# New costs, latencies and conflict units in the list scheduler of a four-layer kernel

## The chip, the cores and the metric

The kernel runs on one core of a Trainium2 chip. The metric is the device time of one execution in microseconds. A NeuronCore has a matrix engine (TensorE, PE in the profile), VectorE (DVE), ScalarE (ACT), GpSimd (POOL) and a queue that issues transfers (SyncE, SP). Each engine works through its own queue in the order in which the program was written, and semaphores make one engine wait for another. The order of each queue is therefore fixed when the program is built.

## The reference, cut to what matters

The input is x, 8 samples of 256 channels by 32 x 32 positions. Four layers follow one another:

```
layer 0: x += gamma1 * attention(rmsnorm(x))        4 heads, keys of 32, values of 64, 1024 positions,
                                                    softmax, a 3x3 depthwise convolution of v added
         x += gamma2 * ffn(rmsnorm(x))              1x1 to 1024, depthwise 3x3, gelu(x1)*x2, 1x1 to 256,
                                                    an 8x8 FFT filter
layer 1: x += attention(groupnorm(x))               8 heads of 32, softmax; then a small gelu MLP
layer 2: quantised 1x1 -> 3x3 -> 1x1 convolutions with a residual
layer 3: a selective scan in four directions (rows, columns, each forward and backward):
         xc, z = split(u W_in);  xc = silu(conv4(xc));  dt, B, C = projections of xc
         h[t] = h[t-1] * exp(dt[t] A) + dt[t] B[t] xc[t]    512 channels x 16 states
         y[t] = sum_s h[t,s] C[t,s];  out = (y + D xc) silu(z) W_out;  the four outputs are added
```

## The kernel before, in words

The kernel has two phases. `phase_a` computes layers 0 to 2, `phase_b` layer 3. Within a phase nothing is a plain loop: the work is written as Python generators ("strands"), and a list scheduler, the class `_Order`, decides in which order their instructions are emitted.

**The list.** A strand yields an `_Op` (one instruction) or a list of them (a group that stays together). `run()` computes for every ready strand when its next group could start (`start()`): when the engine is free, when each operand was last written, and, for what is written, last read. Data from another engine count as usable `LATENCY` after they are finished. The strand with the earliest start is emitted, ties going to the smaller rank, and the engine's free time advances by the group's cost. So the prices in `_Op.__init__` and the latencies shape a simulated timeline at build time, and the order of every queue comes out of it. The chip itself is not told of these times.

**Conflict units.** `_Op.blocks` says which part of a tile an operand touches, in units of 64 elements of a partition for tiles of up to 512 elements, and of 512 for larger ones. Two operands of one tile that share a unit are treated as conflicting in the list.

**Rooms.** Buffers come from rooms (`_Room`). A strand waits until a room has a free buffer; the buffer's earliest use is when its last reader ended, plus a latency (`put`). The PSUM room of `phase_a` is `bank`, with 8 banks; while an attention is running, everything else together may hold three of them (`OTHERS`).

**Fillers.** `keep_dense` runs ahead of every group for PE. It adds up the rows that PE has worked in the last 3.4 us of simulated time. If that is under half of full, it emits filler matmuls (a constant `minus` tile, 128 x 512, priced at 0.22 us, line 277 in the profile) into a free bank. Their purpose is to keep PE's activity up, since the granted clock depends on it. Before the change it may emit as many as fit between the time at which PE is free and the later of two times: the group's expected start, and 0.66 us after PE is free.

**phase_a.** The eight samples run as strands; a sample begins when the one three before it has finished `layer0`. `layer0`, `feed_forward`, `layer1` and `layer2` are the linear parts. `maxima` makes scores in one direction to get each query's maximum and sum: pairs or quads of matmuls into banks (tile names `bank<-big,big`), then for each bank a TENSOR_REDUCE on DVE into one column of `stats` (`least`), then an exponential on ACT with that column as bias, summed into another column of `stats` (`sums`). A `stats` tile has 128 elements to a partition. `exponentials` makes the scores again in the other direction, subtracts maximum and log-sum with a small matmul, takes the exponentials (`exps`), and `values` multiplies them with v.

**phase_b.** The sequence work is cut into 64 blocks (8 samples, 4 directions, 2 halves) with 16 states each: 1024 groups. For each group ACT makes four `dbu` (dt B x, scaled) and four `da` (exp of dt A), PE transposes the `dbu` into `db`, DVE runs four scans into `h` (two to a tile), ACT copies the last column to `st` in the first half of a direction, POOL multiplies `h` by C (`cb`), and PE transposes and sums the products into `py`. The strands `decays`, `scales`, `turns`, `scans`, `ends`, `products` and `sums` do this; `ahead` brings in the projections, convolutions and activations of the blocks to come. `da` has 5 buffers, `dbu` 12, `h` 6 pairs, `db` 3 banks.

Of the kernel before, what the change touches and what calls it, by code (L numbers as in the profile page):

```python
# [20 lines left out]
F32 = mybir.dt.float32  # L21
# [78 lines left out]
class _Op:  # L100


    def __init__(self, engine, method, args, kw):
        self.engine, self.method, self.args, self.kw = engine, method, args, kw
        out, ins = args[0], [a for a in (*args[1:], *kw.values()) if isinstance(a, bass.AP)]
        self.reads = {k for a in ins for k in self.blocks(a)}
        self.writes = {k for a in (out, kw.get("accum_out")) if a is not None for k in self.blocks(a)}
        self.landing = 0.0
        n = max(math.prod(a.shape[1:]) for a in (out, *ins)) / 1024
        near = all(a.space == out.space and out.space != PSUM for a in ins)  # L110
        points = sum(math.prod(a.shape[1:]) == 1 for a in ins)
        if engine == "tensor":
            x = kw.get("rhs", ins[0])
            n = math.prod(x.shape[1:]) / 1024
            self.rows = x.shape[0] / P * n * (0.44 if x.dtype != F32 else 1.72)
            move = method == "transpose" or kw.get("is_transpose", False)
            self.cost = max(0.06, (0.22 if x.shape[0] < 20 else 0) + n * (0.96 if move else 0.44 if x.dtype != F32 else 1.76 if n > 0.2 else 2.0))
            self.rows *= 0.5 if move else 1
        elif engine == "vector":
            fast = near and method in ("tensor_scalar", "tensor_copy")  # L120
            both = near and method == "tensor_tensor"
            three = near and method == "scalar_tensor_tensor"
            if method == "tensor_tensor_scan":
                self.cost = 0.03 + 2.15 * n + 0.05 * points
            elif both or three:
                self.cost = 0.04 + 1.5 * n
            elif fast:
                self.cost = 0.04 + 0.9 * n
            else:
                self.cost = 0.05 + 1.09 * n + 0.05 * points  # L130
        elif engine == "scalar":
            self.cost = 0.05 + 0.06 * near + 0.85 * n + 0.093 * points + 0.17 * ("accum_out" in kw)
        elif engine == "gpsimd":
            self.cost = 0.12 + 2.2 * n if method == "tensor_tensor" else 0.07 + (2.0 if out.dtype == BF16 else 1.5) * n
        else:
            self.cost, self.landing = 0.1, 3.0

    @staticmethod
    def blocks(a):
        step = max(1, a.ap[0][0])  # L140
        lo = a.offset % step
        hi = lo + sum((n - 1) * abs(s) for s, n in list(a.ap)[1:])
        unit = 64 if step <= HALF else HALF
        return [(a.name, k) for k in range(lo // unit, hi // unit + 1)]

    def emit(self, nc):
# [37 lines left out]
class _Order:  # L184
# [2 lines left out]

    LATENCY = 0.35  # L190

    def __init__(self, nc):
        self.nc, self.strands, self.n = nc, [], 0
        self.free, self.written, self.read, self.base, self.last = {}, {}, {}, {}, {}
        self.rooms, self.minus, self.way, self.rows, self.fresh = [], None, 0.0, [], {}

    def add(self, rank, strand):
        self.n += 1
# [30 lines left out]

    def put(self, room, t):  # L230
        k = room.of[t.name]
        end = [v[0] for d in (self.written, self.read) for v in d.pop(t.name, {}).values()]
        self.last[room.tag, k] = max(end + [0.0]) + self.LATENCY
        room.put(t)

    def start(self, ops):
        e = ops[0].engine
        t = self.free.get(e, 0.0)
        for o in ops:
            for k in o.reads | o.writes:  # L240
                t = max(t, self.base.get(k[0], 0.0))
                w, by = self.written.get(k[0], {}).get(k, (0.0, e))
                t = max(t, w + (self.LATENCY if by != e else 0.0))
            for k in o.writes:
                w, by = self.read.get(k[0], {}).get(k, (0.0, e))
                t = max(t, w + (self.LATENCY if by != e else 0.0))
        return t

    WINDOW, DENSE, DUMMY = 3.4, 0.5, 0.22

    def keep_dense(self, t, cost, ops):

        work = sum(o.rows for o in ops)
        free, end = self.free.get("tensor", 0.0), t + cost
        self.rows = [r for r in self.rows if r[1] > end - self.WINDOW]
        seen = sum(w * (b - max(a, end - self.WINDOW)) / (b - a) for a, b, w in self.rows)
        n = math.ceil((self.DENSE * self.WINDOW - seen - work * min(1.0, self.WINDOW / cost)) / self.DUMMY)
        n = max(n, math.ceil((t - free - self.DENSE * self.WINDOW) / self.DUMMY))
        if n > 0:
            since, room, k = min(  # L260
                ((self.last.get((r.tag, k), 0.0), j, k) for j, r in enumerate(self.rooms) for k in r.left),
                default=(1e9, 0, 0),
            )
            x = self.fresh.get(ops[0].args[0].name)
            if x is not None and self.base[x.name] < since:
                since, room = self.base[x.name], None
            begin = max(free, since)
            n = min(n, int((max(t, free + 0.66) - begin) / self.DUMMY))
            if since < 1e9 and n > 0:
                if room is not None:  # L270
                    room = self.rooms[room]
                    room.left.remove(k)
                    room.left.insert(0, k)
                    x = room.take()
                rhs = self.minus.unsqueeze(1).to_broadcast([P, 4, P])
                for _ in range(n):
                    self.nc.tensor.matmul(x, lhsT=self.minus, rhs=rhs, start=True, stop=True)  # L277
                if room is not None:
                    room.put(x)
                    self.last[room.tag, k] = begin + n * self.DUMMY + self.LATENCY  # L280
                self.rows.append((begin, begin + n * self.DUMMY, n * self.DUMMY))
                t = max(t, begin + n * self.DUMMY)
        self.rows.append((t, t + cost, work))
        return t

    def run(self):
        while self.strands:
# [12 lines left out]
            cost, ops = s[2]  # L300
            e = ops[0].engine
            if self.rooms and e == "tensor":
                t = self.keep_dense(t, cost, ops)
            for o in ops:
                o.emit(self.nc)
                for k in o.reads:
# [9 lines left out]
def phase_a(ctx, tc, i, col, ident, codes, w_parts):  # L316
# [18 lines left out]
    order = _Order(nc)  # L335
    NBIG, NMID, NLOW = 12, 9, 7
    OTHERS = 3
    MAXIMA, SCORES = 2, 1.12
    GATE = 1
    big = _Room(rooms, "big", NBIG, [P, CC, N])  # L340
    mid = _Room(rooms, "mid", NMID, [P, N])
# [241 lines left out]
    def maxima(rank, q, k, rows, done):  # L583
# [6 lines left out]
        def some():  # L590
            while todo:
# [9 lines left out]
                for e in range(n):  # L601
# [1 line left out]
                    ops.append(  # L603
                        T.matmul(bb[e], lhsT=q[r, t * P : (t + 1) * P], rhs=k[r, hs(j)], start=True, stop=True)
                    )
                yield (0.9, ops)
                for e in range(n):
                    m, s = (x[:, j, t, h + e : h + e + 1] for x in (least, sums))
                    yield V.tensor_reduce(m, bb[e], AX.X, ALU.max, negate=True)
# [496 lines left out]
        def emit(self, nc):  # L1106
            nc.scalar.preload_act_table_set("natural_log_exp_and_others")

    order.rooms, order.minus, order.way = [bank], minus, 0.05
    stage = [0] * B  # L1110

    def sample(b):
# [670 lines left out]
```

## Time and profile before

| | |
|---|---|
| median of 3 runs | 10249.33 us (10241.9 to 10274.5) |
| profiled execution | 10256.65 us, span 10254.8 us |
| mean granted PE clock | 0.977 |
| busy share of the span | PE 93%, ACT 83%, DVE 75%, POOL 60% |
| filler matmuls (line 277) | 2805, of these 1749 into `bank`, in `phase_a` |

Almost every instruction is emitted by one helper, `_Op.emit`, on line 147, so groups are told apart by engine, operation and tile names. In a group's line come the count, the busy time and the mean of one in ns, then the idle time of the engine just before them and what ended it. Ends of matmuls are modelled, so a busy PE can still be a PE that waits a little; the distance from one start to the next says more. A float32 matmul is recorded as two.

### The profile page before, as it was taken

The page shows a single profiled execution, that of the slowest core. Times are in us where ns is not written, and L with a number is a line of the kernel's source. Part 1 is how long each engine was busy: PE and PEld are TensorE (multiplying, and loading weights), DVE is VectorE, ACT ScalarE, POOL GpSimd, SP SyncE. Part 2 cuts the span into 40 slices and gives each one's busy share as a digit, 9 for nine tenths or more (in the row PEclk, how much of TensorE's full clock was granted, in tenths as well). Part 3 has the DMA queues.
Part 4 walks back from the last instruction along what each step waited for, and adds up shares of the span by engine and source line. Part 5 has one row for each costly group of instructions (what it writes and reads, how often), then busy time and mean ns, then how long its engine had stood idle before and what let it go on. Part 6 is the DMA issues. An engine that isn't in the chain of part 4 may idle for free.

```text
span 10254.8 us, 153646 instructions
## 1 busy us (share of the span) xinstructions
PE 9573.8 (93%) x57349; PEld 5920.9 (58%) x57349; DVE 7741.9 (75%) x8671; ACT 8521.2 (83%) x15873; POOL 6150.3 (60%) x2993
## 2 busy tenths in 40 slices
PE   9999999999999989999999999999999999999998
PEld 3333333333333347777777777777777776777776
DVE  6366557585666448887888888888888888888788
ACT  7867676767666759988998999898999899898898
POOL 1433132242121038877887878787878787787788
PEclk9998999999999999999999999999999999999999
DMA  2100000000000002112111112111111211111111
GB/s 59 30 19 17 21 22 18 17 22 17 17 17 9 17 29 54 52 47 57 44 55 55 47 51 59 44 55 50 54 51 49 55 54 45 59 50 49 55 46 54
DMA packets 219630, 416.06 MB, mean 41 GB/s; under 512 B 25137, under 2 KB 67505, under 8 KB 213762
## 3 DMA queue, kind: packets, MB, share of 16 engines
q1 hardware_dynamic: 218882, 406.24, 13.7%
q8 instruction: 451, 7.39, 0.3%
q14 instruction: 297, 2.43, 0.1%
HBM read 358.43 MB, written 37.22 MB: 39 GB/s over the span
## 4 chain that ended last, share of the span: by engine, by line
ACT 28%; PE 22%; DVE 10%; issue 2%; POOL 1%; DMA 1%; DVEq 0%; SPq 0%; POOLq 0%; ACTq 0%
ACT da L147 11%; ACT dbu L147 10%; PE pp L147 9%; DVE h L147 8%; PE py L147 7%; PE db L147 6%; ACT L147 2%; ACT xs L147 1%; ACT dt L147 1%; DMA wi<-w_in 1%; POOL h L147 1%; ACT L156 1%; DVE ys L147 1%; ACT st L147 1%; ACT z L147 0%
## 5 line engine op out<-in xcount | busy, mean ns | idle before, releaser
L147 POOL TENSOR_TENSOR h<-h,cb 128x1024 f32<-128x1024 f32 x2048 | 4814.7, 2375 | 1013.8 <-DVE h L147 422.9
L147 ACT ACTIVATE da<-dt,am 128x512 f32<-128x512 f32 x4096 | 2863.9, 714 | 506.0 <-DVE h L147 502.0
L147 ACT ACTIVATE dbu<-du,bT 128x512 f32<-128x512 f32 x4096 | 2783.4, 709 | 17.1 <-PE db L147 10.4
L147 DVE TENSOR_TENSOR_SCAN h<-da,db 128x512 f32<-128x512 f32 x2048 | 2342.4, 1202 | 467.1 <-ACT da L147 201.5
L147 DVE TENSOR_TENSOR_SCAN h<-da,st,db 128x512 f32<-128x512 f32 x2048 | 2466.0, 1262 | 224.8 <-ACT da L147 131.3
L147 PE MATMUL db<-ident,dbu 128*128 128x128 f32 x16384 | 2329.7, 276 | 194.7 <-DVE h L147 157.7
L147 PEld LDWEIGHTS db<-ident,dbu 128*128 128x128 f32 x16384 | 1855.6, 141 | 798.8 <-DVE h L147 350.4
L147 PE MATMUL py<-ident,h 128*128 128x128 f32 x16384 | 2099.2, 274 | 95.4 <-POOL h L147 90.0
L147 PEld LDWEIGHTS py<-ident,h 128*128 128x128 f32 x16384 | 1837.4, 141 | 236.4 <-POOL h L147 179.2
L147 DVE TENSOR_REDUCE stats<-bank 128x1 f32<-128x512 f32 x1536 | 987.9, 684 | 655.0 <-PE bank L147 652.2
L147 ACT ACTIVATE bank<-bank,stats 128x512 f32<-128x512 f32 x1536 | 1024.7, 672 | 409.2 <-DVE stats L147 395.3
L147 POOL TENSOR_TENSOR mid<-mid,mid 128x961 f32<-128x961 f32 (+2 forms) x192 | 394.6, 2062 | 1115.5 <-ACT mid L147 591.9
L147 PE MATMUL bank<-big,big 32*128 32x512 f32 x4096 | 928.3, 667 | 15.7 <-ACT bank L147 9.0
L147 ACT ACTIVATE exps<-bank 128x512 f32<-128x512 f32 x1536 | 796.9, 620 | 166.4 <-PE bank L147 158.9
L147 PE MATMUL pp<-xi,cvd 128*128 128x512 f32 x1488 | 692.6, 601 | 1.6 <-DVE ys L147 1.6
L277 PEld LDWEIGHTS <-minus 128*128 128x128 bf16 x2805 | 260.6, 101 | 663.4 <-issue 463.8
L147 DVE SCALAR_TENSOR_TENSOR mid<-mid,cols,mid 128x961 f32<-128x961 f32 (+1 forms) x384 | 595.6, 1551 | 6.1
L277 PE MATMUL bank<-minus 128*128 128x512 bf16 x1749 | 508.5, 414 | 52.5 <-ACT bank L147 41.1
L147 PEld LDWEIGHTS bank<-big,big 32*128 32x128 f32 x4096 | 283.2, 191 | 463.0 <-issue 267.4
L147 PE MATMUL bank<-exps,big 128*32 128x512 f32 (+1 forms) x3072 | 543.8, 613 | 0.3 <-ACT exps L147 0.3
L147 POOL TENSOR_TENSOR tmp<-dt,xs 128x512 f32<-128x512 f32 x256 | 322.6, 1274 | 298.2 <-ACT dt L147 227.0
L147 POOL TENSOR_TENSOR big<-big,mid 128x992 f32<-128x992 f32 (+1 forms) x128 | 324.4, 2542 | 290.1 <-ACT mid L147 287.4
(207 smaller groups left out, 9389.5 us busy)
## 6 DMA issues: line engine op xcount, KB each, us to landing
cb<-c_d SPq DMA_DIRECT2D x1024, 256.0 KB, 3.3
wi<-w_in SPq DMA_DIRECT2D x192, 192.0 KB, 3.6
big<-in_x_dram SPq DMA_DIRECT2D x16, 1024.0 KB, 5.2
kept<-big SPq DMA_DIRECT2D x16, 1024.0 KB, 3.9
big<-kept SPq DMA_DIRECT2D x16, 1024.0 KB, 4.8
xf<-codes SPq DMA_DIRECT2D x48, 256.0 KB, 4.0
big<-big SPq DMA_DIRECT2D x16, 512.0 KB, 6.7
codes<-low SPq DMA_DIRECT2D x32, 256.0 KB, 2.0
```

What stands on the lines that cost most here:

```text
L147: return getattr(getattr(nc, self.engine), self.method)(*self.args, **self.kw)
L156: nc.scalar.preload_act_table_set("natural_log_exp_and_others")
L277: self.nc.tensor.matmul(x, lhsT=self.minus, rhs=rhs, start=True, stop=True)
```

## The change

Only the list changes; the instructions of the computation stay as they are.

- Prices of instructions get new constants, for most a few per cent from the old ones; a matmul with under 20 rows loses a surcharge of 0.22 us, and a float32 transpose goes from 0.96 to 0.854 us for 1024 columns.
- `LATENCY` is no longer 0.35 us for all, but 0.06 to 0.21 us by the engine that produced the data. A transfer counts 3.6 us to its landing, 3.0 before.
- Tiles of up to 256 elements to a partition are tracked by single elements.
- `advance` is new: the list keeps account of PE's work in windows of 3.4 us and lets PE run at half pace in the window after one that was under 37.5% full.
- `keep_dense` emits fillers only as far as they fit before the expected start of the group; the 0.66 us are gone.
- A group of scores costs 1.29 us (1.12), a pair or quad of `maxima` 1.06 or 0.96 us (0.9), and a group of matmuls in `phase_a` gets 0.1 us on top (0.05).

```diff
         if engine == "tensor":
...
-            self.rows = x.shape[0] / P * n * (0.44 if x.dtype != F32 else 1.72)
+            self.rows = x.shape[0] / P * n * (0.427 if x.dtype != F32 else 1.707)
...
-            self.cost = max(0.06, (0.22 if x.shape[0] < 20 else 0) + n * (0.96 if move else 0.44 if x.dtype != F32 else 1.76 if n > 0.2 else 2.0))
+            self.cost = max(0.05, n * (0.427 if x.dtype != F32 else 0.854 if move else 1.707))
...
             elif both or three:
-                self.cost = 0.04 + 1.5 * n
+                self.cost = 0.04 + 1.53 * n
             elif fast:
-                self.cost = 0.04 + 0.9 * n
+                self.cost = 0.04 + 0.87 * n
             else:
-                self.cost = 0.05 + 1.09 * n + 0.05 * points
+                self.cost = 0.05 + 1.12 * n + 0.06 * min(points, 1)
         elif engine == "scalar":
-            self.cost = 0.05 + 0.06 * near + 0.85 * n + 0.093 * points + 0.17 * ("accum_out" in kw)
+            self.cost = 0.04 + 0.054 * near + 0.852 * n + 0.093 * points + 0.1 * ("accum_out" in kw)
         elif engine == "gpsimd":
-            self.cost = 0.12 + 2.2 * n if method == "tensor_tensor" else 0.07 + (2.0 if out.dtype == BF16 else 1.5) * n
+            self.cost = 0.12 + 2.3 * n if method == "tensor_tensor" else 0.07 + (2.0 if out.dtype == BF16 else 1.5) * n
         else:
-            self.cost, self.landing = 0.1, 3.0
+            self.cost, self.landing = 0.06, 3.6
...
-        unit = 64 if step <= HALF else HALF
+        unit = 1 if step <= 256 else 64 if step <= HALF else HALF
...
-    LATENCY = 0.35
+    LATENCY = {"tensor": 0.21, "vector": 0.12, "scalar": 0.14, "gpsimd": 0.1, "sync": 0.06}
...
-                t = max(t, w + (self.LATENCY if by != e else 0.0))
+                t = max(t, w + (self.LATENCY[by] if by != e else 0.0))
...
+    def advance(self, t, cost, work):
+
+        while True:
+            while self.window < int(t / self.WINDOW + 1e-9):
+                self.half = self.dense < 0.375 * self.WINDOW
+                self.window, self.dense = self.window + 1, 0.0
+            pace = 0.5 if self.half else 1.0
+            end = (self.window + 1) * self.WINDOW
+            part = min(cost, (end - t) * pace)
+            self.dense += work * part / cost if cost else 0.0
+            work -= work * part / cost if cost else 0.0
+            cost -= part
+            t += part / pace
+            if cost < 1e-6:
+                return t
+            t = end + 1e-6
...
-            n = min(n, int((max(t, free + 0.66) - begin) / self.DUMMY))
+            n = min(n, int((t - begin) / self.DUMMY))
...
-        self.rows.append((t, t + cost, work))
-        return t
+        end = self.advance(t, cost, work)
+        self.rows.append((t, end, work))
+        return t, end - t
...
-    MAXIMA, SCORES = 2, 1.12
+    MAXIMA, SCORES = 2, 1.29
...
-                yield (0.9, ops)
+                yield (0.96 if n > 2 else 1.06, ops)
...
-    order.rooms, order.minus, order.way = [bank], minus, 0.05
+    order.rooms, order.minus, order.way = [bank], minus, 0.1
```

## The prediction

> **What bounds the kernel now.** I read the page's busy table first (PE 93%, ACT 83%, DVE 75%, POOL 60%), then the windows, because an average hides two halves: the last `bank` instruction ends and the first `db` one starts near 3698 us, so phase_a is 0 to 3698 and phase_b the rest.
>
> ```profile
> 0.00:3698.00 3698.00, 3492.14 (x15717) 1243.67 (x15717) 2204.74 (x3294) 2635.27 (x5724) 924.96 (x476) 0.94 0.07 21
> 3698.00:10254.80 6556.80, 6081.71 (x41632) 4677.24 (x41632) 5537.15 (x5377) 5885.96 (x10150) 5225.36 (x2518) 1.00 0.18 51
> ```
>
> After the length come PE, PEld, DVE, ACT, POOL (busy us, count), clock, DMA. In phase_a PE is busy for 94% at a clock of 0.94, ACT for 71%, DVE for 60%: PE sets the time. A PE granted only 1 or 0.5 that averages 0.94 spent 2 x 0.06 x 3698 = about 440 us at half clock. In phase_b nothing is full: PE 93%, ACT 90%, DVE 84%, POOL 80%.
>
> Not all of PE's time is wanted. The same windows for L277 alone, the filler matmuls of `keep_dense`:
>
> ```profile
> 0.00:3698.00 3698.00, 508.54 (x1749) 156.24 (x1749) 0.94 0.07 21
> 3698.00:10254.80 6556.80, 270.58 (x1056) 104.36 (x1056) 1.00 0.18 51
> ```
>
> PE's timeline shows what they do to the path. Here PE alternates between pairs of score matmuls of `maxima` (each is recorded as two, hence x4) and fillers, without a gap:
>
> ```profile
> 1323.29 0.39 PE L277 MATMUL bank<-minus 128*128 128x512 bf16 x1
> 1323.61 1.13 PE L147 MATMUL bank<-big,big 32*128 32x512 f32 x4
> 1324.67 0.82 PE L277 MATMUL bank<-minus 128*128 128x512 bf16 x3
> 1325.42 1.13 PE L147 MATMUL bank<-big,big 32*128 32x512 f32 x4
> 1326.48 0.60 PE L277 MATMUL bank<-minus 128*128 128x512 bf16 x2
> ...
> 957.43 2.08 PE L147 MATMUL bank<-big,big 32*128 32x512 f32 x4
> 959.44 1.03 PE L277 MATMUL bank<-minus 128*128 128x512 bf16 x2
> 960.40 2.08 PE L147 MATMUL bank<-big,big 32*128 32x512 f32 x4
> ```
>
> From start to start, a pair takes 1.06 us and a run of 1, 2, 3 fillers 0.32, 0.54, 0.75 us: 0.11 + 0.215 n. The last three lines are the same work at half clock (2.01 us a pair), where it stayed for 51 us although fillers stood between all pairs: too few to lift the density, they only cost time.
>
> Why does the list put them there? It expected gaps. `stats` has 128 numbers to a partition; in units of 64 all `least` of a tile are one unit, so the list made each TENSOR_REDUCE wait until the exponential before it had read its own number. By its prices one value costs 0.595 + 0.35 + 0.738 + 0.35 = 2.03 us, and 1536 values 3120 us along a single tile. The chip does not wait so: three reduces take 1.89 us in a row.
>
> ```profile
> 1301.43 1.89 DVE L147 TENSOR_REDUCE stats<-bank 128x1 f32<-128x512 f32 x3 [2.11 <-PE bank L147]
> ```
>
> Two groups of the page:
>
> ```profile
> L147 DVE TENSOR_REDUCE stats<-bank 128x1 f32<-128x512 f32 x1536 | 987.9, 684 | 655.0 <-PE bank L147 652.2
> L147 ACT ACTIVATE bank<-bank,stats 128x512 f32<-128x512 f32 x1536 | 1024.7, 672 | 409.2 <-DVE stats L147 395.3
> ```
>
> DVE's idle time (after the second bar) before the reduces is nearly all for PE, so PE is the late one.
>
> Phase_b's largest waits, 4000 to 10000 us:
>
> ```profile
> ACT da L147 <- DVE h L147: 484.3, 398, 4.8
> POOL h L147 <- DVE h L147: 401.9, 330, 5.1
> DVE h L147 <- ACT da L147: 319.0, 66, 7.6
> ```
>
> They close a ring (da, scan, da's buffer free again), and the order in the queues decides how long they are.
>
> **What the Trainium skill says.** (1) "TensorE: Matmul & The Clock Gate", section "Part 1: The HAM clock gate", gives a free-running window of 3413 ns and two rates, full and half. The trace agrees: PEclk is 0.50 in 975 to 1008. (2) Its section "HAM oscillation" prices throttled time at one half; the pairs agree (2.01 against 1.06 us). (3) Its "Back-to-back issue gap" has about 216 ns for 512 columns; fillers here step by 215. (4) "Perfetto Trace Analysis", "Per-instruction lifecycle", says that a DVE or ACT record runs on to the write acknowledgement, so a record is longer than its slot. The trace agrees (684 ns a record, 0.60 us from start to start), so the new ACT and DVE prices, below the records, are near the slots.
>
> **The change, part by part.** No instruction of the computation is added or removed; queue orders and the number of fillers change.
>
> *Fillers without an expected gap.* `max(t, free + 0.66)` allowed up to three (3 x 0.22) where the list saw no gap. In the PE timeline from 100 to 3600 us I count 337 runs of one to three with 697 fillers, 117 longer ones with 906. If all the short ones go: 697 x 0.215 + 337 x 0.11 = 187 us. Some will stay in real gaps: 80%, **150 us**. PE is the queue that sets the end of phase_a, so all of it counts, unless the clock takes it back.
>
> *Single numbers as units, latencies by engine.* The list's step for a value falls from 2.03 us to its dearest engine, 0.66 us. Expected gaps shrink, and with them the longer runs: of their 906 x 0.215 + 117 x 0.11 = 208 us I take 45%, **95 us**. (All: 208. None, if the gaps have other causes: 0.)
>
> *Clock.* What fillers held up falls back. A pair alone carries 2 x 0.25 x 0.86 = 0.43 us of rows in 1.06 us, 40% of a window; the list's own mark is 37.5%. Pairs slowed to ACT's 1.32 us for two exponentials are below it (33%). `advance` sees half windows but, a slowed PE having no gap, `keep_dense` then adds nothing. Against that, filler-less pairs at half clock (2.01 us) cost about the 1.8 us of a pair with three at full clock. I take half-clock time from 440 to 540 us: **50 us lost**. Bounds: 200 us less (100 gained) and 1000 us more (500 lost).
>
> *Order in phase_a.* Maxima are started earlier against attention, and banks come free sooner in the list. PE's real gaps there are about 170 us in 3500 (start-to-start beyond the usual); I take **25 us**, bounds -80 to +80.
>
> *Phase_b.* 161 of its 233 filler runs have one to three, 235 in all: 235 x 0.215 + 161 x 0.11 = 68 us of PE; with ACT as loaded as PE a third is on the path, **20 us**. Latency 0.35 to 0.12 for DVE matches the trace: three scans of 1.12 us start at 6006.70, the waiting da starts at 7.95, 0.13 after the first ends. The ring is thus ordered more truly; of 484 us I take 5%, **25 us**. Against this stand POOL's 2.42 us for a product (its slot is 2.35: 4.71 for two) and transposes at 0.427 us for four with no allowance for changing groups in phase_b. Bounds for the whole of phase_b: 150 gained, 130 lost.
>
> *Cost at nothing:* the DMA's 3.66 for 3.1 us (the page's landings are 3.3 to 6.7; PE and its weight loads wait for `wi` some 40 us in all), SCORES and the pairs' new prices (they only shift expected times, counted under order), the tail 3636 to 3698, a chain without choice. SP's and POOL's queues get the same instructions.
>
> Sum: 150 + 95 - 50 + 25 + 20 + 25 = 265 us. The profiled execution took 10256.65 us (span 10254.8), 7.3 over the median 10249.33. From the execution 9992; from the median 9984. I say **9990 us**.
>
> **Rivals.** *The clock takes it back (slower).* Fewer fillers, far more half windows. Each us at half clock costs half a us of PE; with 265 + 50 = 315 us gained otherwise, it decides from 630 us more, 1070 in all. At 1250: 315 - 405, so 10340 us. For it: low-density pairs are in every sample, and one half stretch lasted 51 us. Against: all work other than pairs is dense[...].
>
> *Phase_b gets worse.* A list mispricing POOL and transposes queues ring members wrongly; at 1.5% of 6557 us that is +100 against -220: 10130 us, still faster. At +4% it would end slower, too.
>
> *Same.* PE's freed time turns into waits, the banks or ACT being just behind it: 10250 us. Against: ACT is idle for 29% and DVE for 40% of phase_a.
>
> *More.* All long runs go and the clock holds (-187 - 208), and phase_b gains 80: about 9775 us.
>
> *The change does nothing:* excluded by the code, which must move fillers.
>
> **How the numbers follow.** My case 0.53 (own range 9870 to 10110), more 0.14, phase_b worse but net faster 0.11: faster 0.78. Same 0.06. Slower 0.16, nearly all by the clock. 0.3% is 31 us, about what a measurement can tell from no change. The range, 9780 to 10310, leaves out about 0.1 at each end.
>
> **What would show it.** L277 in phase_a well below 1749, to 700 to 1000, runs of one to three mostly gone; phase_a ending near 3480; its clock 0.91 to 0.94; phase_b 6510, with under 900 fillers and a smaller wait of da for h. I am wrong if phase_a's clock falls below 0.85, if DVE's idle time before the reduces goes to ACT while phase_a stays at 3700, or if phase_b moves by over 150 us.

## The result and the profile after

The changed kernel takes 10141.26 us (median of 4 executions) against 10259.51 us for the kernel before (4 as well): a ratio of 0.9884, 95% interval 0.9864 to 0.9903. It is faster by 118 us where the prediction said 259. The profiled executions are 10143.13 and 10256.65 us, 113.5 us apart, and the windows of the two phases say where.

From here on phase_a ends with its last `bank` instruction: 3679 us before (the prediction drew the line at the first `db` instruction, 3698), 3584 us after. Phase_b is the rest: 6576 before, 6557 after. So **phase_a gained 95 us** (220 forecast: 150 + 95 - 50 + 25) and **phase_b 19 us** (45 forecast).

The windows of the kernel after (length; PE, PEld, DVE, ACT, POOL busy us and count; clock; DMA share; GB/s), the two phases:

```profile
0.00:3584.00 3584.00, 3337.93 (x15141) 1217.98 (x15142) 2311.69 (x3273) 2618.88 (x5731) 963.65 (x479) 0.94 0.07 22
3584.00:10141.30 6557.30, 6034.17 (x41391) 4697.26 (x41510) 5548.15 (x5391) 5897.93 (x10150) 5234.04 (x2522) 0.99 0.17 52
```

The same windows for the fillers alone (they sit on line 295 now):

```profile
0.00:3584.00 3584.00, 343.18 (x1174) 96.46 (x1174) 0.94 0.07 22
3584.00:10141.30 6557.30, 230.89 (x934) 93.37 (x934) 0.99 0.17 52
```

Fillers in phase_a fell from 1749 to 1174, and the clock stayed at 0.94. But the short runs stayed too: 323 runs of one to three with 632 fillers, where the kernel before had 344 with 713. The long ones went: 54 with 542, where it had 130 with 1036. PE's timeline after, the same kind of place as the one shown before, and beside it ACT's:

```profile
2164.60 1.13 PE L147 MATMUL bank<-big,big 32*128 32x512 f32 x4
2165.66 0.39 PE L295 MATMUL bank<-minus 128*128 128x512 bf16 x1
2165.98 1.13 PE L147 MATMUL bank<-big,big 32*128 32x512 f32 x4
2167.04 0.61 PE L295 MATMUL bank<-minus 128*128 128x512 bf16 x2
2167.58 1.13 PE L147 MATMUL bank<-big,big 32*128 32x512 f32 x4
```

```profile
2166.55 0.66 ACT L147 ACTIVATE bank<-bank,stats 128x512 f32<-128x512 f32 x1
...
2167.22 0.65 ACT L147 ACTIVATE bank<-bank,stats 128x512 f32<-128x512 f32 x1
...
2167.89 0.66 ACT L147 ACTIVATE bank<-bank,stats 128x512 f32<-128x512 f32 x1
...
2168.55 0.66 ACT L147 ACTIVATE bank<-bank,stats 128x512 f32<-128x512 f32 x1
```

ACT starts an exponential every 0.66 to 0.67 us here, without a pause. A pair needs two, 1.33 us, and PE needs only 1.06, so 0.27 us of each gap are real and PE does not set the pace at this place. A run of two fillers takes 0.54 us, though: PE's step is then 1.60 us, more than ACT's 1.33, and a little later DVE waits for PE:

```profile
2173.52 1.29 DVE L147 TENSOR_REDUCE stats<-bank 128x1 f32<-128x512 f32 x2 [0.46 <-PE bank L147]
```

Over the whole program the idle time before these two steps fell, but it did not vanish: before the reduces from 655 to 443 us, nearly all of it for PE, and before the exponentials from 409 to 208 us. The page after:

```profile
L147 DVE TENSOR_REDUCE stats<-bank 128x1 f32<-128x512 f32 x1536 | 973.1, 681 | 443.2 <-PE bank L147 441.0
L147 ACT ACTIVATE bank<-bank,stats 128x512 f32<-128x512 f32 x1536 | 1029.2, 679 | 208.3 <-DVE stats L147 194.3
```

**A ledger for phase_a.** From the PE timeline and the clock records I took, for every run of this study, the fillers' time at full rate (start to start) and half of the time at half clock. Both together stand for what PE pays for its clock; the rest is the work and the waits. This is an account and not a measurement: it takes each us at half clock for half a us lost, whether PE was needed just then or not.

```
us, profiled execution          phase_a  fillers  their time  half clock/2  both  rest
before                             3679     1749         422           207   628  3051
after                              3584     1174         292           200   492  3092
gap clause alone (e1)              3699     1599         383           261   644  3055
after, no fillers (e3)             3608        0           0           519   519  3089
before, no fillers (e4)            3715        0           0           593   593  3122
group prices alone (f1)            3593     1526         372           157   529  3064
the same, nudged (h2)              3723     1581         383           278   661  3062
best (f4)                          3431      959         241           142   383  3048
```

Over all 20 profiled executions the rest stays between 3027 and 3122 us, while "both" runs from 383 to 690 us and goes with the length of phase_a at a correlation of 0.95 (in part by construction, since the length is "both" plus the rest). The change saved 130 us of fillers and 7 us of clock, and the rest grew by 41 us: 95 us gained, rounded. By the windows PE stood idle for 246 us of phase_a after and for 187 us before, so its waits are long enough to account for the 41.

### The profile page after: what moved, and what is told of

Read it like the earlier page. It is cut to its first block, busy times and chain, and to the rows that moved or that the text cites. A ratio compares the mean times of both kernels' runs of the same rounds, so it can differ in the third digit from the quotient of the medians.

```text
span 10141.3 us, 152451 instructions
## 1 busy us (share of the span) xinstructions
PE 9372.1 (92%) x56530; PEld 5915.2 (58%) x56652; DVE 7859.8 (78%) x8663; ACT 8516.8 (84%) x15881; POOL 6197.7 (61%) x3001
## 4 chain that ended last, share of the span: by engine, by line
PE 27%; ACT 22%; DVE 11%; issue 3%; DMA 1%; POOL 1%; DVEq 0%; SPq 0%; POOLq 0%; ACTq 0%
PE pp L147 12%; DVE h L147 9%; ACT da L147 9%; PE py L147 8%; PE db L147 8%; ACT dbu L147 7%; ACT L147 2%; ACT xs L147 1%; ACT dt L147 1%; DMA wi<-w_in 1%; ACT L156 1%; DVE du L147 1%; POOL h L147 1%; ACT st L147 0%; DVE ys L147 0%
## 5 line engine op out<-in xcount | busy, mean ns | idle before, releaser
L147 POOL TENSOR_TENSOR h<-h,cb 128x1024 f32<-128x1024 f32 x2048 | 4812.4, 2374 | 972.8 <-DVE h L147 442.2
L147 ACT ACTIVATE da<-dt,am 128x512 f32<-128x512 f32 x4096 | 2873.5, 714 | 450.6 <-DVE h L147 442.0
L147 ACT ACTIVATE dbu<-du,bT 128x512 f32<-128x512 f32 x4096 | 2800.6, 709 | 55.3 <-PE db L147 50.5
L147 PE MATMUL db<-ident,dbu 128*128 128x128 f32 x16384 | 2402.0, 278 | 386.8 <-DVE h L147 333.1
L147 DVE TENSOR_TENSOR_SCAN h<-da,db 128x512 f32<-128x512 f32 x2048 | 2344.1, 1201 | 441.2 <-ACT da L147 182.5
L147 DVE TENSOR_TENSOR_SCAN h<-da,st,db 128x512 f32<-128x512 f32 x2048 | 2464.5, 1260 | 262.6 <-ACT da L147 153.6
L147 PEld LDWEIGHTS db<-ident,dbu 128*128 128x128 f32 x16384 | 1872.5, 142 | 948.3 <-DVE h L147 523.4
L147 PE MATMUL py<-ident,h 128*128 128x128 f32 x16384 | 2096.4, 274 | 33.3 <-POOL h L147 32.4
L147 PEld LDWEIGHTS py<-ident,h 128*128 128x128 f32 x16384 | 1850.3, 141 | 96.7 <-POOL h L147 54.5
L147 DVE TENSOR_REDUCE stats<-bank 128x1 f32<-128x512 f32 x1536 | 973.1, 681 | 443.2 <-PE bank L147 441.0
L147 ACT ACTIVATE bank<-bank,stats 128x512 f32<-128x512 f32 x1536 | 1029.2, 679 | 208.3 <-DVE stats L147 194.3
L147 POOL TENSOR_TENSOR mid<-mid,mid 128x961 f32<-128x961 f32 (+2 forms) x192 | 418.6, 2187 | 983.1 <-ACT mid L147 778.4
L147 PE MATMUL bank<-big,big 32*128 32x512 f32 x4096 | 898.3, 648 | 19.6 <-ACT bank L147 12.1
L147 ACT ACTIVATE exps<-bank 128x512 f32<-128x512 f32 x1536 | 802.1, 641 | 111.5 <-PE bank L147 101.6
L147 PE MATMUL pp<-xi,cvd 128*128 128x512 f32 x1488 | 688.0, 598 | 6.3 <-DVE dt L147 6.3
L147 DVE SCALAR_TENSOR_TENSOR mid<-mid,cols,mid 128x961 f32<-128x961 f32 (+1 forms) x384 | 651.4, 1696 | 7.7
L147 PE MATMUL bank<-exps,big 128*32 128x512 f32 (+1 forms) x3072 | 566.0, 624 | 4.9 <-ACT exps L147 4.8
L147 PEld LDWEIGHTS bank<-big,big 32*128 32x128 f32 x4096 | 293.8, 187 | 465.4 <-issue 250.3
L147 POOL TENSOR_TENSOR tmp<-dt,xs 128x512 f32<-128x512 f32 x256 | 322.8, 1272 | 320.2 <-ACT dt L147 206.9
L147 POOL TENSOR_TENSOR big<-big,mid 128x992 f32<-128x992 f32 (+1 forms) x128 | 331.6, 2598 | 305.2 <-ACT mid L147 302.6
L147 POOL TENSOR_SCALAR big<-big,ga,gs 128x512 f32<-128x512 f32 x64 | 70.0, 1106 | 728.3 <-issue 325.3
L147 PE MATMUL bank<-big 32*128 32x512 f32 x2048 | 455.7, 667 | 38.7 <-ACT mid L147 11.3
```

The source lines that it names most:

```text
L147: return getattr(getattr(nc, self.engine), self.method)(*self.args, **self.kw)
```

## The experiments

The two phases have separate lists, so each run tests one edit in each; a switch at the start of the phase sets it, and the diffs give in short what the switch does. Lines are numbered a little differently in these kernels (L181 or L178 for L147). Durations of phases are those of the profiled execution; "by medians" means the median of the runs less phase_b and less the 1.9 us between span and execution. One execution of phase_a is not sharp: the four executions of h2 lie between 10052 and 10155 us, at clocks of 0.978 and 0.967, and the kernel before, run again beside each group of experiments, had medians from 10250 to 10278 us. Phase_b is sharper: the one list of it that was profiled twice (e7 and f4) took 6418 us both times.

**e1: the gap clause alone, both phases, on the kernel before.**

```diff
-            n = min(n, int((max(t, free + 0.66) - begin) / self.DUMMY))
+            n = min(n, int((t - begin) / self.DUMMY))
```

> The kernel before with one edit: fillers only as far as they fit before the expected start (the 0.66 us are gone), in both phases. The prediction held that 80% of the short runs (one to three) exist only by that clause: then about 550 of the 713 short fillers of phase_a go, PE saves 150 us there, and phase_a ends near 3550 us instead of 3698. The rival: the short runs stand in gaps that the list expects in any case (the pairs wait for ACT's exponentials), so nearly all stay: over 1500 fillers in phase_a, phase_a shorter by 10 to 40 us, the whole kernel by under 50 us. In phase_b both expect about 100 fillers fewer, worth 0 to 20 us.

Measured: ratio 1.0031 (1.0020 to 1.0043). Phase_a 3699 us, phase_b 6583. The fillers' group on the page and the window of phase_a:

```profile
L333 PE MATMUL bank<-minus 128*128 128x512 bf16 x1599 | 472.8, 423 | 41.0 <-ACT bank L181 26.1 <-ACT exps L181 10.0 <-POOL eps L425 1.6
```

```profile
0.00:3699.00 3699.00, 3513.91 (x15567) 1254.19 (x15567) 2207.78 (x3282) 2632.65 (x5722) 919.39 (x470) 0.93 0.06 21
```

150 fillers fewer, as the rival said, and not one us gained: the fillers' time fell by 39 us, and half-clock time rose from 413 to 522 us, worth 54. Of the 713 short fillers 621 stayed, in gaps that the list expects in any case. In phase_b 102 fillers went, and it took 7 us more. The step that I priced at 150 us is worth nothing or a little less.

**e2: phase_a with units, latencies and gap clause; phase_b with the new instruction prices alone.**

```diff
@@ phase_a, on the kernel before @@
-        unit = 64 if step <= HALF else HALF
+        unit = 1 if step <= 256 else 64 if step <= HALF else HALF
-    LATENCY = 0.35
+    LATENCY = {"tensor": 0.21, "vector": 0.12, "scalar": 0.14, "gpsimd": 0.1, "sync": 0.06}
-            n = min(n, int((max(t, free + 0.66) - begin) / self.DUMMY))
+            n = min(n, int((t - begin) / self.DUMMY))
@@ phase_b, on the kernel before: the whole price part of _Op @@
```

> phase_a: the kernel before with single elements as units, the latencies by engine, and the gap clause; prices, half-clock account and the prices of score groups stay old. If the units and latencies carry the change in phase_a, it ends near 3604 us as in the changed kernel, with about 1350 fillers. If prices and the half-clock account matter as much, it ends at 3640 to 3680. phase_b: the kernel before with the new prices alone. If prices carry the little gain there, phase_b takes 6538 us as in the changed kernel; if the latencies do, it stays at 6557.

Measured: ratio 0.9833 (0.9812 to 0.9855). Phase_a 3637 us. **Phase_b 6439 us, 137 less than before and 118 less than in the changed kernel.** The ring of da and the scans shows in the waits of 4000 to 9880 us (us in total, times, longest); first the kernel after, then e2:

```profile
ACT da L147 <- DVE h L147: 422.0, 364, 5.6
POOL h L147 <- DVE h L147: 412.4, 343, 5.8
DVE h L147 <- ACT da L147: 314.2, 65, 6.3
```

```profile
ACT da L181 <- DVE h L181: 306.5, 336, 4.1
POOL h L181 <- DVE h L181: 208.2, 212, 3.5
DVE h L181 <- ACT da L181: 211.4, 51, 6.3
```

After, the ring waits nearly as long as before the change; with the new prices alone all three waits are shorter by a quarter to a half. So something else in the change takes most of the gain of the prices back.

**e3 and e4: no fillers.** e3 is the changed kernel without fillers in both phases. e4 has phase_a of the kernel before without fillers, and phase_b of the kernel before with the new latencies alone.

```diff
@@ e3, phase_a (e4 the same, with the kernel before's 0.05) @@
-    order.rooms, order.minus, order.way = [bank], minus, 0.1
+    order.rooms, order.minus, order.way = [], minus, 0.1
@@ e3, phase_b @@
-    order.rooms = [ps_room, pp_room]
+    order.rooms = []
```

> The changed kernel with no fillers in either phase (and with that no half-clock account, which sits in the same call). If fillers are on PE's path and the clock stands without them, phase_a loses their 316 us of PE time and ends at 3300 to 3400 us. If the clock takes it back, half-clock time rises from 400 us; it breaks even at 400 + 2 x 316 = 1030 us, and above it phase_a is longer than 3604 us. If PE's freed time turns into waits for ACT and DVE, phase_a ends at 3560 to 3620 with the clock near 0.94. In phase_b, where no engine is full, 0 to 60 us shorter, or longer by half of the half-clock time added.

Measured: ratio to before 0.9975 (0.9966 to 0.9983). Windows:

```profile
0.00:3608.00 3608.00, 3295.20 (x13968) 1324.13 (x13968) 2287.90 (x3272) 2622.59 (x5733) 970.76 (x481) 0.86 0.07 22
3608.00:10221.50 6613.50, 5955.90 (x40577) 4703.57 (x40576) 5559.62 (x5390) 5911.84 (x10150) 5233.51 (x2522) 0.96 0.17 51
```

The clock of phase_a is 0.86: half-clock time went from 399 to 1038 us (the ledger's 519, doubled), and phase_a ends 24 us later (43 by medians). 292 us of filler time and 319 us of lost clock weigh nearly the same. In phase_b the fillers do pay: 56 us longer without them, at a clock of 0.96.

> phase_a: the kernel before with no fillers, old order otherwise. The same three cases as for the changed kernel: fillers on the path (474 us of PE time gone, phase_a near 3300 us), clock (half-clock time above 410 + 2 x 474 = 1360 us, phase_a longer than 3698 us), waits (phase_a near 3650). Its distance to the changed kernel without fillers is what the order alone is worth in phase_a: the prediction had 25 us; if the order got worse by the 60 us that PE waits more, this one is the shorter. phase_b: the kernel before with the new latencies alone: 6557 us if the latencies do nothing, 6530 to 6540 if they carry the gain.

Measured: ratio 1.0172 (1.0152 to 1.0193). Phase_a 3715 us, 36 longer than with fillers, 107 longer than e3 (94 by medians). So the gain of the change is there without any filler, and comes from the order; by the ledger 74 of the 107 us are lost clock that this order avoids. **Phase_b with the new latencies alone: 6716 us, 140 longer than before.** Its da waits for h went up to 562 us in the same window.

**e5 to e8: single parts taken out of the changed phase_a, single latencies put into phase_b.** Each phase_b is the kernel before with the new prices and 0.35 us, except where the diff says otherwise.

```diff
@@ e5, phase_a, on the changed kernel @@
-    LATENCY = {"tensor": 0.21, "vector": 0.12, "scalar": 0.14, "gpsimd": 0.1, "sync": 0.06}
+    LATENCY = 0.35
@@ e5, phase_b @@
+    LATENCY = 0.5
@@ e6, phase_a, on the changed kernel @@
-        unit = 1 if step <= 256 else 64 if step <= HALF else HALF
+        unit = 64 if step <= HALF else HALF
@@ e6, phase_b @@
+    LATENCY["vector"] = 0.12
@@ e7, phase_a, on the changed kernel: advance() returns t + cost at once @@
@@ e7, phase_b @@
+    LATENCY["scalar"] = 0.14
@@ e8, phase_a, on the changed kernel: the old price part of _Op @@
@@ e8, phase_b @@
+    LATENCY["tensor"] = 0.21
```

> phase_a: the changed kernel with the old latency of 0.35 us for all. If the true latencies are what makes its order better, phase_a goes back towards 3640 or more (last bank instruction; changed kernel 3584, before 3679); if latencies cost there as they did alone in phase_b (+140), it ends at 3540 to 3570. phase_b: the kernel before with the new prices and a latency of 0.5 us for all. Theory M, a margin: a list whose expected times run ahead of the chip puts waiting instructions too early into the queues, and a long latency covers that; then 6400 to 6450, no longer than the 6439 of new prices with 0.35. Theory T, truth: 0.35 was a compensation that fits by accident, further off is worse: 6480 or more. Theory C, chance: any edit reshuffles phase_b by 100 us either way, and nothing follows.

> phase_a: the changed kernel with units of 64 again. If the single-number units carry the gain of phase_a, it goes back to 3650 to 3680 (changed 3584); if the other parts do, it stays under 3610. phase_b: the kernel before with new prices, latency 0.35 us except DVE's, 0.12. The da ring (da, scan, da) goes through DVE's latency: if a short DVE latency is the harmful one, 6500 to 6560; if not, near 6439.

> phase_a: the changed kernel without the half-clock account. If it matters (the list knows when PE is slow), phase_a loses 20 to 60 us against 3584; if not, 3570 to 3600. phase_b: the kernel before with new prices, latency 0.35 us except ACT's, 0.14. If a short latency behind ACT (da to scan, st to product, dbu to transpose) is the harmful one, 6500 to 6560; if not, near 6439.

> phase_a: the changed kernel with the old prices of single instructions (the prices of score groups stay new). If the prices matter as in phase_b (137 us of 6576, 2%), phase_a loses 50 to 80 us against 3584; if not, within 20. phase_b: the kernel before with new prices, latency 0.35 us except PE's, 0.21. If a short PE latency is the harmful one, 6500 to 6560; if not, near 6439. Theory M expects every one of the three single short latencies to cost 0 to 120 us, about 120 in sum; theory C expects signs of both kinds.

```
      ratio to before (95%)       phase_a, by medians   phase_b
e5    0.9703 (0.9687-0.9720)      3479                  6477   all 0.50
e6    0.9857 (0.9838-0.9876)      3576                  6537   DVE 0.12
e7    0.9693 (0.9676-0.9710)      3527                  6418   ACT 0.14
e8    0.9686 (0.9659-0.9714)      3451                  6495   PE 0.21
```

Phase_b: against 6439 us, the short latency behind DVE costs 98 us, behind PE 56, and behind ACT it gains 21. Their sum, 133, is about what the changed kernel has over e2 (118). Longer than 0.35 is no better (+38), so theory M in its simple form falls: of the values tried, 0.35 us is the best. Phase_a: with the units of 64 back it is as long as in the changed kernel (3576 against 3582 by medians). Leaving out the latencies, the half-clock account or the prices makes it shorter, by 103, 55 and 131 us; a loss of 20 to 80 us was expected for the last two, if they mattered.

**f1 to f4: group prices alone, nudges, and the best of both.** A nudge is an edit without meaning, 0.01 us on a latency.

```diff
@@ f1, phase_a, on the kernel before @@
-    MAXIMA, SCORES = 2, 1.12
+    MAXIMA, SCORES = 2, 1.29
-                yield (0.9, ops)
+                yield (0.96 if n > 2 else 1.06, ops)
-    order.rooms, order.minus, order.way = [bank], minus, 0.05
+    order.rooms, order.minus, order.way = [bank], minus, 0.1
@@ f1, phase_b; f2, phase_a: both on the kernel before @@
-    LATENCY = 0.35
+    LATENCY = 0.36
@@ f2, phase_b, with the new prices @@
-    LATENCY = 0.35
+    LATENCY = 0.36
@@ f3, both phases, on the changed kernel @@
+    LATENCY["gpsimd"] = 0.11
@@ f4: phase_a of e8, phase_b of e7 @@
```

> phase_a: the kernel before with only the new prices of score groups (1.29 us, 1.06 or 0.96 us, and 0.1 us on a group). Among the earlier runs the lists with these prices ended between 3474 and 3584 us, those without between 3637 and 3699. If these prices carry the gain, this one ends under 3620; if not, at 3650 to 3700. phase_b: the kernel before with all latencies at 0.36 instead of 0.35 us, an edit without meaning. Theory C (chance): phase_b moves by 50 us or more from 6576; theory of causes: by under 30.

> phase_a: the kernel before with latencies of 0.36 us. phase_b: new prices with 0.36 us for all. Both are nudges without meaning. If differences of 50 to 100 us are causes, phase_a stays within 25 us of 3679 and phase_b within 30 us of 6439. If they are chance, one of them moves by 50 us or more.

> The changed kernel with GpSimd's latency at 0.11 instead of 0.10 us: a nudge. If the changed kernel's 3584 us in phase_a is a poor draw among orders that its list could as well have given, phase_a moves, most likely down to 3480 to 3550. If each of its new parts really costs time there (each left out singly gave 0 to 110 us), it stays within 25 us. phase_b: within 30 us of 6557 if the short latencies of DVE and PE are its cause, else anywhere from 6420 to 6600.

> The two best phases so far put together: phase_a as the changed kernel with old instruction prices (3474 us in its run), phase_b with new prices, 0.35 us of latency for all engines but ACT, 0.14 (6418 us). The phases have separate lists, so the times should add: 9892 us of span, 0.964 of the kernel before. If they disturb each other, more than 20 us above that.

Measured: f1 0.9898 (0.9883 to 0.9913), phase_a 3593; f2 0.9823 (0.9807 to 0.9838), phase_a 3648; f3 0.9879 (0.9863 to 0.9896), phase_a 3596. Phase_b under the nudges: 6576, 6433 and 6561 us against 6576, 6439 and 6557. They move it by 0 to 6 us, and the nudge of h1 below by 19, so its differences of 38 us and more can be put down to the edits; the 21 us of ACT's latency cannot. f4 is the fastest kernel of the study: 9871.74 us, ratio **0.9606 (0.9585 to 0.9627)**. Its windows:

```profile
0.00:3431.00 3431.00, 3232.19 (x14926) 1185.18 (x14927) 2224.19 (x3276) 2624.99 (x5728) 939.20 (x476) 0.96 0.07 23
3431.00:9848.90 6417.90, 5986.27 (x41322) 4669.93 (x41457) 5540.98 (x5391) 5881.02 (x10150) 5238.09 (x2522) 0.99 0.18 53
```

Its phase_a has the same list as e8's, and took 43 us less in its profiled execution: half-clock time was 283 us here and 389 there. By medians the two agree, 3452 and 3451 us.

**g1 to g4: why the short latencies lose in phase_b, and whether phase_a's parts add.** g1 and g4 have, in phase_b, new prices and new latencies with one price corrected; g2 has 0.5 us behind DVE alone; g3 is e7's phase_b with the scan's price raised.

```diff
@@ g1 and g3, phase_b @@
-                self.cost = 0.03 + 2.15 * n + 0.05 * points
+                self.cost = 0.05 + 2.15 * n + 0.05 * points
@@ g2, phase_b @@
+    LATENCY["vector"] = 0.5
@@ g4, phase_b @@
-            self.cost = 0.12 + 2.3 * n if method == "tensor_tensor" else 0.07 + (2.0 if out.dtype == BF16 else 1.5) * n
+            self.cost = 0.12 + 2.2 * n if method == "tensor_tensor" else 0.07 + (2.0 if out.dtype == BF16 else 1.5) * n
@@ phase_a @@
@@ g1: the changed kernel with old prices and old latencies @@
@@ g2, g3, g4: f1 and the new latencies; f1 and the units; f1 and the new prices (POOL's product at the old one) @@
```

> phase_b: new prices and new latencies, and the price of a scan raised by 0.02 us (1.125 and 1.175 us; seven took 7.89 us). If the short DVE latency loses because the list's scans are ahead of the chip's, phase_b falls from about 6557 to 6430 to 6470. If the margin itself is what helps, it stays at 6530 to 6580. phase_a: the changed kernel with old instruction prices and old latencies both. Left out singly they gave 131 and 103 us against 3582 (medians: 3451 and 3479); if both losses are separate causes, 3350 to 3400; if they are one thing (expected times too short for the chip), 3440 to 3500.

> phase_b: new prices, 0.35 us for all but DVE, 0.5. With DVE at 0.12 it was 6537, at 0.35 6439, and with all at 0.5 6477. If longer is better behind DVE (margin), 6380 to 6430; if 0.35 is near the best, 6430 to 6480. phase_a: the kernel before with group prices (3593 alone) and the new latencies: if the latencies lose there as well, 3640 to 3700; if they only lose beside the new instruction prices, 3550 to 3610.

> phase_b: new prices, ACT 0.14 and the others 0.35 us (6418), with the scan's price raised by 0.02 us. If a truer scan helps by itself, 6380 to 6410; if not, within 20 of 6418. phase_a: the kernel before with group prices and single-number units: if the units help where the group prices are right, 3520 to 3570; if they are worth nothing, as when left out of the changed kernel, 3580 to 3600.

> phase_b: new prices and new latencies, but POOL's product at the old 2.32 us (two took 4.71). If POOL's too long price makes the short latencies lose, 6430 to 6480; if not, 6540 to 6570. phase_a: the kernel before with group prices and new instruction prices: if these lose as they did in the changed kernel, 3640 to 3720; if only beside the new latencies, 3570 to 3610.

```
      ratio to before (95%)       phase_a, by medians   phase_b
g1    0.9831 (0.9810-0.9852)      3561                  6528
g2    0.9984 (0.9975-0.9993)      3756                  6487
g3    0.9718 (0.9701-0.9736)      3553                  6422
g4    0.9883 (0.9865-0.9902)      3586                  6557
```

Phase_b: the truer scan wins back 29 of the 118 us, not much more than a nudge, the truer product none. g4 also shows the loss with prices and latencies alone: its phase_b has neither the units nor the half-clock account nor the gap clause, and takes the changed kernel's 6557 us. And 0.5 us behind DVE alone costs 48 us against 0.35. Neither of these two prices nor "more margin is better" explains the best value. Phase_a: its parts don't add. New latencies beside the group prices lose 163 us (g2), inside the whole change 103 (e5), and where the prices of single instructions are old they gain 110 (e8 against g1). The units beside the group prices gain 40 (g3), the new prices 7 (g4).

**h1 and h2: nudges of the results that matter for phase_a.**

```diff
@@ h1, phase_a, on f4 @@
+    LATENCY["gpsimd"] = 0.11
@@ h1, phase_b, on f4: 0.36 for 0.35, ACT 0.15 for 0.14 @@
@@ h2, phase_a, on f1 @@
-    LATENCY = 0.35
+    LATENCY = 0.36
@@ h2, phase_b, new prices @@
+    LATENCY = {"tensor": 0.35, "vector": 0.35, "scalar": 0.14, "gpsimd": 0.1, "sync": 0.06}
```

> The fastest combination with nudges: phase_a with GpSimd's latency 0.11 instead of 0.10 us, phase_b with 0.36 instead of 0.35 and ACT 0.15 instead of 0.14 us. If phase_a's 3452 us (median less phase_b) is a cause, it stays within 35 us; if it is a lucky draw, it ends at 3500 to 3600. phase_b within 15 us of 6418.

> phase_a: group prices alone with latencies of 0.36 instead of 0.35 us. If their gain of about 100 us is a cause, it ends within 35 us of 3593; if a draw, up to 3690. phase_b: new prices with the new latencies of ACT, POOL and SP (0.14, 0.10, 0.06 us) and 0.35 us for PE and DVE: if only the latencies of PE and DVE lose, 6400 to 6430.

Measured: h1 0.9662 (0.9639 to 0.9685), phase_a 3510 by medians, 58 more than f4; phase_b 6399. h2 0.9851 (0.9797 to 0.9904), phase_a 3678, **85 more than f1**; phase_b 6430, so the short latencies of ACT, POOL and SP lose nothing there. The 85 us are themselves not sharp: two executions of h2 took 10052 and 10064 us, two 10154 and 10155, and its median lies between them. By medians the four nudges of phase_a moved it by 10, 45, 58 and 85 us. So f1's gain cannot be called an effect of the group prices, and no difference under some 90 us between two lists of phase_a can be called an effect of the part that was edited. The gain of the whole change in phase_a, 95 us, is hardly above this mark: the changed kernel and its nudge lie at 3582 and 3592 by medians, the kernel before and its nudge at 3700 and 3655, so that the edits cause the gain is likely, but a lucky draw among orders is not excluded. What stands is f4's kind of order: with its nudge, at 3452 and 3510, it is well below the kernel before and its nudge.

## Why the prediction was wrong, point by point

The sign was right and the size was not: 118 us of the forecast 259. By its own steps:

- **Fillers without an expected gap, 150 us: the step that failed.** I took the short runs for forced ones. In the change 81 of 713 short fillers went, and 21 of 344 runs: about 20 us at the prediction's own prices (0.215 us a filler, 0.11 a run). With the clause alone gone (e1), 621 of them stayed, because the list expects a gap there in any case; a part of it is real, 1.33 us on ACT against 1.06 us on PE for a pair.
- **"... all of it counts, unless the clock takes it back": the premise under this step failed too.** In e1 the clock's loss grew by 54 us against 39 us of filler time saved; as half-clock time also moves by as much between a list and its nudge (314 and 556 us, f1 and h2), e1 alone would prove little. But without any filler, 292 us of filler time turn into 319 us of lost clock (e3). I had set the clock beside the sum as a side cost; it is the other half of the same bill, and only an order that needs fewer fillers for the same clock gains. The term itself, 50 us lost, came out as 7 us gained, because the short fillers stayed.
- **Single numbers as units, latencies by engine, 95 us: right for the fillers, not shown for the time.** The long runs lost 494 fillers, 48% where I took 45%, about 115 us; the ledger has 130 us for short and long runs together. Either part is enough: of the lists with fillers, every one with the units or the new latencies has 426 to 647 fillers in long runs, every one with neither 745 to 1107, and a nudge moves the count by 71 at most. But the length of phase_a does not follow the count: with 647 (g2) it took 3755 us, the longest of all, and with the units of 64 back (e6, 492) it is as long as in the changed kernel. That the whole gain came to 95 us as well is chance.
- **Order in phase_a, 25 us gained: 41 us lost** in waits, by the ledger. This is the rival "Same" in part: PE's freed time turned into waits. 130 + 7 - 41 is the 95 us, rounded.
- **Phase_b, 45 us: 19 came, as the difference of two large terms that I did not see.** The fillers, 20 us: the clause alone gained none (e1). The new prices gain 137 us; I had them only as a risk. The new latencies, which I credited with 25 us because they match the trace, lose 118 beside the new prices and 140 beside the old. The match is true as far as it goes: over some 670 waits in the changed kernel, transposes that waited for a scan start 1.31 us after its start (median), and the list expected 1.105 or 1.155 + 0.12, 0.03 to 0.09 less than that; the old latency expected 0.15 to 0.2 us more. The truer one gives the worse order. That DVE's and PE's latencies do it is shown; why 0.35 is better than 0.12 and 0.5 stays open. A scan priced 2% too low accounts for 29 us of it at most.
- The rival of the clock was the right one to name: its price of half a us for each us fits (the rest is 3092 us with fillers and 3089 without, e3), and its break-even of 630 us more at half clock was not reached, since the fillers that stayed held the clock. With all of them gone it is 639 more.
- The rival "phase_b gets worse by mispriced POOL and transposes" is refuted for POOL (g4) and, as a whole, by e2: the new prices are what gained. A loss of its size was there all the same, in the latencies.
- A misreading without effect: the landings on the page start at 2.0 us (`codes<-low`), not at 3.3.

Which part of the change makes phase_a's order better stays open. The runs speak against the gap clause (alone, no gain) and the units (left out, no loss) as its cause, though with nudges of up to 85 us they do not exclude them; for the others, nudges move phase_a as much as most parts do.

## What to carry to other kernels

When an order comes out of a list scheduler, measure the parts of a recalibration one by one and nudge each winner with an edit that means nothing: here a nudge moved one phase by 19 us at most and the other by up to 85, and only the first can be explained part by part. Fillers that hold a clock are no free time to win back: add their time and half of the half-clock time, and look for an order that lowers the sum. Truer latencies need not give a better order; here, in phase_b, truer prices gained and truer latencies lost, and the change kept both.

## What the runs showed of the hardware

- Holding the clock with fillers and letting it fall cost nearly the same in phase_a: 3584 us at a clock of 0.94 with 1174 fillers, 3608 us at 0.86 with none.
- Fillers did not always lift the clock. In the kernel before it stayed at half from 957 to 1008 us with one to four fillers between the pairs and PE busy throughout, and was full again after a run of eight. What the clock counts is not shown. Its changes lie on one grid of 3.413 us, to 0.02 us, in the traces of both kernels (119 changes before, 169 after).

```profile
1003.31 2.08 PE L147 MATMUL bank<-big,big 32*128 32x512 f32 x4
1005.32 3.52 PE L277 MATMUL bank<-minus 128*128 128x512 bf16 x8
1008.77 1.14 PE L147 MATMUL bank<-big 32*128 32x512 f32 x8
```

- One and the same program can differ by 103 us between executions (10052 to 10155 us, h2), with the granted clock at 0.978 and 0.967; another by 49 us (e8, 9922 to 9971 us, at 0.983 and 0.976).
